# Where the product of px with the decays is made: one VectorE instruction, or four scaled copies on ScalarE

## The chip, the core and the metric

The kernel runs on one core of one Trainium2 chip, in one launch. The metric is the device time of that launch in microseconds (us), as a median over several runs. The core has five engines with queues of their own, each of which runs its instructions in the order of the program: TensorE (PE in the profile; its weight loads are PEld), VectorE (DVE), ScalarE (ACT), GpSimd (POOL) and SyncE (SP), which here only issues DMAs. They wait for one another through semaphores. Matmuls write to PSUM, of which a tile of 128 x 512 floats fills one bank; everything else that the engines share lies in SBUF.

## What is computed

The reference is one block of a network: layer norm, an attention layer, a residual sum, layer norm, a feed-forward layer with weights from a table of 16 values, a residual sum. The attention layer is a gated delta rule with 32 value heads of width 128 over 4 sequences of 1024 rows, in chunks of 64 rows. What matters here, cut from it (one head, one chunk; `Tm` is the inverse of a triangular matrix):

```python
u = Tm @ v_beta
kcd = Tm @ (k_beta * jnp.exp(gc)[..., None])
def step(St, inp):
    q_i, k_i, u_i, kcd_i, dec_i, g_i = inp
    attn = (q_i @ k_i.T) * dec_i
    v_new = u_i - kcd_i @ St
    inter = (q_i * jnp.exp(g_i)[..., None]) @ St
    out_i = inter + attn @ v_new
    g_last = g_i[..., -1]
    St_new = St * jnp.exp(g_last) + (k_i * jnp.exp(g_last - g_i)[..., None]).T @ v_new
    return St_new, out_i
```

So the new values of a chunk, `v_new`, are used twice: by the chunk's own output, and, scaled row by row with the decay from that row to the chunk's end, by the sum that updates the state `St`.

## The kernel before

**Tiling.** Heads are worked in 8 groups of 4. A *unit* is one chunk of two sequences for the 4 heads of a group: 2 x 64 rows fill the 128 partitions, and the 4 heads lie beside each other, 128 columns each, in one tile of 128 x 512 (`t4`, one PSUM bank). Eight units make a *super*; there are 4 supers in a group, 32 supers and 256 units in all. Units alternate between two pairs of sequences, so there are two running states, `S`.

**The order of the work** is written out by hand. `SLOTS` (lines 859 to 868) has one line for each unit of a super; each letter resumes one generator, and what it records goes at once to the end of the queues of the engines that it uses. In the order of a slot:

- `A` and `B`: `channel`, the projections of one tile of values (`A`) and of queries or keys (`B`) with a convolution: 8 matmuls `pp`, a scaled copy `cv` on ACT (line 437), three multiply-adds `cv` on DVE (line 440), a Silu on ACT (line 444).
- `N0`, `N1`, `N2`, `O3`, `J`, `O4`: the six parts of `step`, one unit. `N0` transposes the values (`pv`) and copies them, scaled, to `x0` on ACT (line 675). `N1` multiplies queries and keys with the state (`pkqs`), adds to `x0` on DVE (line 695) and makes `qs` on ACT (line 696: four copies, one for each head, scaled by a column). `N2` multiplies `x0` with the inverse: `px`, which is minus `v_new`, up to the scales; from it ACT makes `xs` (line 709), and line 712 makes `yg`, its product with the decays `ncd`; PE transposes the keys (`pk`), ACT copies them to `kt` (line 717), and POOL multiplies the state with its decay (line 721). The next unit's slot goes on: `O3` makes `po` from `xs` and `core` on DVE, `J` four sums of squares on ACT (`junk`), `O4` multiplies `kt` with `yg` (`pu`) and DVE adds that to the state (line 748).
- `T`, `Z`, `U`: `project_out`: gates (`pz`, a Silu `zs` on ACT, two products `zs` on POOL, lines 784 and 786), transposes (`pto`, `oT`), the output projection (`pout`, `ac`).
- `v1`: one step of `invert`, an inversion by substitution on DVE, two instructions with all operands in SBUF (`rank` and `v`, lines 580 and 581), 31 steps a super, spread over units 7 and 0 to 3 mostly.
- `n`, `s`, `b`, `r`, `q`: `norms`, `scores` (decays `dc` on POOL and ACT), `build`, `rms`, `roots`. In the slots with `r` and `q` ACT needs Sqrt and then Exp, and Silu again after that, and a table is loaded for each.

**Buffers.** Tiles from `bank` share four PSUM banks in turn: a matmul into the fifth tile waits until the readers of the first are done. In most slots the tiles come as px, pk, pout, po, pv, pto, pkqs, pkqs, pz (and kkq or others between), so `pz` takes the bank of `pv`, which is free when `x0` has been copied. Tiles `pp` and `pu` share two double banks. `px` is read twice, by `xs` and by `yg`, and its bank is free after both; the two readers run one after the other.

**What the change touches:** line 712 in `step`. `ncd` is a small tile made by `norms`, one column for each head of each unit; `bc` repeats a column along 128 elements. `last` is true in the last two units of a group, where there is no state to update; so line 712 runs in 240 of the 256 units.

Of the kernel before, what the change touches and what calls it, by code (L numbers as in the profile page):

```python
# [11 lines left out]
AF = mybir.ActivationFunctionType  # L12
ALU = mybir.AluOpType
# [10 lines left out]
HG = 4  # L24
# [35 lines left out]
def bc(ap, shape):  # L60
    return ap.to_broadcast(shape)
# [3 lines left out]
def delta_net_ffn_kernel(  # L65
# [18 lines left out]
    V, A, G_, T_ = nc.vector, nc.scalar, nc.gpsimd, nc.tensor  # L84
# [7 lines left out]
    def bank(name):  # L92
        return psum.tile([P, 512], F32, tag="ps", name=name)

    def two_banks(name):
        return psum2.tile([P, 2, 512], F32, tag="pp", name=name)
# [97 lines left out]
    with tc.tile_pool(name="pre", bufs=2) as pre, tc.tile_pool(name="gates", bufs=1) as gp:  # L194
# [38 lines left out]
        u = gp.tile(full, F32, name="u")  # L233
# [75 lines left out]
    with ExitStack() as main:  # L309
# [6 lines left out]
        def t4(name, bufs=1):  # L316
            return sc.tile([P, HG, P], F32, tag=name, name=name, bufs=bufs)

        h4 = [P, HG, P]

        def as4(ps):
            return ps.rearrange("p (h i) -> p h i", h=HG)
# [335 lines left out]
        def step(k, u):  # L658

            blk, un = divmod(u, 4)  # L660
            n, p = divmod(un, 2)
            ti = k.t0 + u
            ex, _, _, _, el = dks[k.g]
            first = k.first and u < 2
            last = k.last and u >= SB - 2
            S_ = states[p]
            qk, vt = k.qku.pop(u), k.vt[blk]

            pv = bank("pv")
            for h in range(HG):  # L670
                T_.transpose(as4(pv)[:, h, :], vt[h][:, un * P : (un + 1) * P], ident)
            x0 = t4("x0")
            for m in range(MG):
                two = slice(2 * m, 2 * m + 2)
                A.activation(x0[:, two, :], as4(pv)[:, two, :], AF.Copy, scale=k.nnk[:, u, m : m + 1])
            yield
            if not first:
                got = []
                for j in range(2):
                    ps = bank("pkqs")  # L680
                    for m in range(MG):
                        two = slice(2 * m, 2 * m + 2)
                        for ab in range(2):
                            T_.matmul(  # L684
                                as4(ps)[ab * C : (ab + 1) * C, two, :],
                                lhsT=qk[:, m, j, ab, :],
                                rhs=S_[:, ab, two, :],
                                start=True,
                                stop=True,
                            )  # L690
                    got.append(ps)
                qs = t4("qs")
                for h in range(HG):
                    e = ex[:, ti, h : h + 1]
                    V.scalar_tensor_tensor(x0[:, h, :], as4(got[0])[:, h, :], e, x0[:, h, :], ALU.mult, ALU.add)
                    A.activation(qs[:, h, :], as4(got[1])[:, h, :], AF.Copy, scale=e)
            yield

            ue, ae = k.exp.pop(u)

            def applied(w, src, name):
                ps = bank(name)
                for h in range(HG):
                    T_.matmul(as4(ps)[:, h, :], lhsT=w[:, h, :], rhs=src[:, h, :], start=True, stop=True)  # L704
                return ps

            px = applied(ue, x0, "px")
            xs = t4("xs")
            A.activation(xs, as4(px), AF.Copy, scale=-1.0)  # L709
            if not last:  # L710
                yg = t4("yg")
                V.tensor_tensor(yg, as4(px), bc(k.ncd[:, u, :].unsqueeze(2), h4), ALU.mult)
                pk = bank("pk")
                for m in range(MG):
                    T_.transpose(as4(pk)[:, m, :], qk[:, m, 0].rearrange("p a t -> p (a t)"), ident)
                kt = sc.tile([P, MG, P], F32, tag="kt", name="kt")
                A.copy(kt, as4(pk)[:, :MG, :])
                if not first:
                    flat = S_.rearrange("p a h d -> p (a h) d")
                    decay = el[:, ti].rearrange("p a h -> p (a h)").unsqueeze(2)  # L720
                    G_.tensor_tensor(flat, flat, bc(decay, [P, 2 * HG, P]), ALU.mult)  # L721
            yield
            po = applied(ae, xs, "po")
            core = t4("core", OUT_LAG)
            if first:
                V.tensor_copy(core, as4(po))
            else:
                V.tensor_tensor(core, as4(po), qs, ALU.add)  # L728
            k.cores[u] = core
            yield  # L730
            junk = sc.tile([P, P], F32, tag="junk", name="junk")
            for h in range(HG):
                A.activation(junk, core[:, h, :], AF.Square, accum_out=k.ms[:, u, h : h + 1])  # L733
            yield
            if not last:
                pu = two_banks("pu")
                for m in range(MG):
                    two = slice(2 * m, 2 * m + 2)
                    for ab in range(2):
                        half = slice(ab * C, (ab + 1) * C)  # L740
                        T_.matmul(  # L741
                            as4(pu[:, ab])[:, two, :], lhsT=kt[half, m, :], rhs=yg[half, two, :], start=True, stop=True
                        )
                state = S_.rearrange("p a h d -> p (a h d)")
                if first:
                    V.tensor_copy(state, pu.rearrange("p a n -> p (a n)"))
                else:
                    V.tensor_tensor(state, pu.rearrange("p a n -> p (a n)"), state, ALU.add)
# [274 lines left out]
        with tc.manual_schedule(engines=COMPUTE):  # L1023
            for s in range(-LQ, len(units)):
                n, i = divmod(s, SB)
                nq, iq = divmod(s + LQ, SB)
                nv, iv = divmod(s + LV, SB)
                gens = {}
                newer = step(*units[s]) if s >= 0 else None
                for c in "01234":  # L1030
                    gens["N" + c], gens["O" + c] = newer, older
# [127 lines left out]
```

## Time and profile before

| | us |
|---|---|
| median of 3 runs | 4344.73 |
| lowest and highest run | 4342.15 to 4349.24 |
| the profiled execution | 4347.06 |
| its span on the core | 4345.3 |
| chain that ended last: PE, DVE, ACT | 57%, 25%, 6% of the span |
| PE idle ahead of `px` (line 704) | 168.2 |
| DVE idle ahead of `cv` (line 440), until ACT's `cv` (line 437) | 322.7 |
| ACT idle ahead of `cv` (line 437), until PE's `pp` | 486.0 |

How to read it: the time of the runs holds a little more than the span, which goes from the first to the last instruction on the core. The chain is followed back from the last instruction, at each step to what released it or to its predecessor on its engine. Idle time of an engine that is not the bottleneck costs nothing. A row of a group reads: line, engine, operation, output<-inputs, shape, count | busy us, mean ns of one | idle us just before them, and what ended most of it. A row of the timeline reads: start us, length us, engine, line, operation, output<-inputs, shape, count, and in brackets the engine's idle time just before it with what ended that. A row of the windows reads: from:to, length, then for each engine its busy time and number of instructions, the granted clock of TensorE, the share of the DMA engines and GB/s.

### The profile page before, as it was taken

The numbers are of one execution on the slowest core, as the hardware profiler recorded it, in microseconds if no ns is written. First come the engines' busy times: TensorE is split into PE (matmuls) and PEld (weight loads), VectorE is DVE, ScalarE is ACT, GpSimd is POOL, SyncE is SP. The second block draws the span as 40 slices with busy tenths as digits, with TensorE's granted clock in tenths as the row PEclk, the third lists the DMA queues.
The fourth block names the chain that finished last, engine by engine and source line by source line (L and its number), as shares of the span: only waits on it lengthen the run. The fifth ranks groups of instructions, "written<-read, shape, count | busy, mean of one in ns | idle before, by whom it ended". The sixth has DMA issues, their size and how long they took to land.

```text
span 4345.3 us, 79442 instructions
## 1 busy us (share of the span) xinstructions
PE 3992.3 (92%) x26664; PEld 2858.5 (66%) x26664; DVE 3517.0 (81%) x6641; ACT 2646.9 (61%) x6573; POOL 2082.5 (48%) x1782
## 2 busy tenths in 40 slices
PE   3679999999999999999999999999999999999999
PEld 3456667677666666676766667676766776666454
DVE  4788888888888888888888988888888898886243
ACT  2456667666666666666666666666666666656211
POOL 2545564655555554655455554555554343434122
PEclk7899999999999999999999999999999999999999
DMA  3444444444444454444454444544445444443011
GB/s 88 124 107 113 111 112 124 121 130 119 126 130 118 107 133 125 134 117 119 125 135 128 109 114 128 133 118 114 132 128 128 115 120 121 130 108 96 26 39 29
DMA packets 1053124, 492.72 MB, mean 113 GB/s; under 512 B 730528, under 2 KB 951856, under 8 KB 1052720
## 3 DMA queue, kind: packets, MB, share of 16 engines
q1 hardware_dynamic: 1052720, 487.64, 42.5%
q8 instruction: 216, 3.54, 0.3%
q14 instruction: 188, 1.54, 0.1%
HBM read 267.66 MB, written 219.69 MB: 112 GB/s over the span
## 4 chain that ended last, share of the span: by engine, by line
PE 57%; DVE 25%; issue 7%; ACT 6%; POOL 3%; DMA 1%; SPq 1%; DVEq 0%; POOLq 0%; ACTq 0%
PE pp L423 13%; DVE cv L440 9%; PE pout L797 7%; PE pz L143 7%; PE pkqs L684 6%; DVE rank L580 4%; PE pgu L960 4%; PE px L704 4%; PE pu L741 3%; PE po L704 3%; DVE v L581 2%; PE kkq L546 2%; PE py L976 2%; DVE core L728 2%; PE pto L790 1%
## 5 line engine op out<-in xcount | busy, mean ns | idle before, releaser
L440 DVE SCALAR_TENSOR_TENSOR cv<-pp,cw,cv 128x512 f32<-128x512 f32 x1536 | 1148.9, 748 | 352.2 <-ACT cv L437 322.7
L784 POOL TENSOR_TENSOR zs<-zs,rr 128x512 f32<-128x512 f32 x256 | 267.0, 1043 | 1558.3 <-ACT zs L782 1549.3
L437 ACT ACTIVATE cv<-pp,cw 128x512 f32<-128x512 f32 x512 | 350.9, 685 | 486.0 <-PE pp L423 486.0
L581 DVE TENSOR_TENSOR v<-v,rank 128x31 f32<-128x31 f32 (+15 forms) x992 | 553.3, 558 | 34.1
L423 PE MATMUL pp<-xnT,wq 128*128 128x262 f32 x2048 | 531.0, 401 | 43.3 <-DVE cv L440 34.6
L423 PEld LDWEIGHTS pp<-xnT,wq 128*128 128x128 f32 x2048 | 371.7, 191 | 216.6 <-issue 58.7
L423 PE MATMUL pp<-xnT,wv 128*128 128x262 f32 x2048 | 503.0, 387 | 5.8 <-DVE cv L440 5.8
L797 PE MATMUL pout<-wo,oT 128*128 128x256 f32 x2048 | 504.9, 391 | 0.7 <-ACT oT L792 0.7
L143 PE MATMUL pz<-wzs,xnT 128*64 128x512 f32 x2048 | 487.1, 596 | 4.7 <-DVE ac L802 3.8
L580 DVE TENSOR_TENSOR rank<-v,lb 128x31 f32<-128x31 f32 (+15 forms) x992 | 467.2, 471 | 25.9 <-DMA lb<-ltd 20.1
L684 PE MATMUL pkqs<-S,qku 128*64 128x256 f32 x3840 | 478.1, 387 | 5.2 <-DVE core L728 3.5
L721 POOL TENSOR_TENSOR S<-S,dkm 128x1024 f32<-128x1024 f32 x224 | 436.7, 1949 | 26.5 <-PE pkqs L684 16.1
L704 PE MATMUL px<-x,ue 128*128 128x128 f32 x2048 | 292.9, 287 | 168.2 <-issue 108.1
L704 PEld LDWEIGHTS px<-x,ue 128*128 128x128 f32 x2048 | 264.1, 194 | 269.0 <-issue 151.1
L423 PEld LDWEIGHTS pp<-xnT,wv 128*128 128x128 f32 x2048 | 381.5, 190 | 73.8 <-issue 13.1
L797 PEld LDWEIGHTS pout<-wo,oT 128*128 128x128 f32 x2048 | 384.1, 198 | 49.4 <-issue 3.4
L684 PEld LDWEIGHTS pkqs<-S,qku 128*64 128x64 f32 x3840 | 248.7, 136 | 204.2 <-issue 49.2
L733 ACT ACTIVATE junk<-core 128x128 f32<-128x128 f32 x1024 | 318.5, 311 | 82.4 <-DVE core L728 53.9
L786 POOL TENSOR_TENSOR zs<-zs,core 128x512 f32<-128x512 f32 x256 | 328.6, 1284 | 20.0
L709 ACT ACTIVATE xs<-px 128x512 f32<-128x512 f32 x256 | 154.8, 605 | 236.2 <-PE px L704 236.2
L444 ACT ACTIVATE qk<-cv 128x512 f32<-128x512 f32 x256 | 161.2, 630 | 206.1 <-DVE cv L440 202.6
L741 PE MATMUL pu<-yg,kt 64*128 64x256 f32 x1920 | 272.2, 402 | 14.5 <-DVE cv L440 13.1
(187 smaller groups left out, 7198.4 us busy)
## 6 DMA issues: line engine op xcount, KB each, us to landing
qkd<-qk SPq DMA_DIRECT2D x256, 256.0 KB, 2.6
qku<-qkd SPq DMA_DIRECT2D x256, 256.0 KB, 2.9
dc<-rows_d SPq DMA_DIRECT2D x256, 128.0 KB, 3.4
ltd<-lT SPq DMA_DIRECT2D x128, 256.0 KB, 2.5
atd<-aT SPq DMA_DIRECT2D x128, 256.0 KB, 2.8
ae<-atd SPq DMA_DIRECT2D x512, 64.0 KB, 2.6
acc_d<-ac SPq DMA_DIRECT2D x256, 128.0 KB, 2.2
ac<-acc_d SPq DMA_DIRECT2D x224, 128.0 KB, 2.6
```

Of the source, the lines that this page charges most:

```text
L143: T_.matmul(ps[ab * C : (ab + 1) * C, :], lhsT=xnT[:, kc, 2 * p + ab, H + n * C : H + (n + 1) * C], rhs=rhs(kc), start=kc == 0, stop=kc == ...
L423: T_.matmul(ps[:, 2 * p : 2 * p + 2, : H + BT], lhsT=wt[:, kc, :], rhs=xnT[:, kc, 2 * p : 2 * p + 2, c0 : c0 + H + BT], start=kc == 0, sto ...
L437: A.activation(cv, ps[:, :, H : H + BT], AF.Copy, scale=cw[:, ch, H : H + 1])
L440: V.scalar_tensor_tensor(cv, ps[:, :, i : i + BT], cw[:, ch, i : i + 1], cv, ALU.mult, ALU.add)
L580: V.tensor_tensor(t, bc(v[:, 0 : j + 1, j : j + 1], sh), bc(lb[:, j : j + 1, j + 1 :], sh), ALU.mult)
L581: V.tensor_tensor(v[:, 0 : j + 1, j + 1 :], v[:, 0 : j + 1, j + 1 :], t, ALU.subtract)
L684: T_.matmul(as4(ps)[ab * C : (ab + 1) * C, two, :], lhsT=qk[:, m, j, ab, :], rhs=S_[:, ab, two, :], start=True, stop=True,)
L704: T_.matmul(as4(ps)[:, h, :], lhsT=w[:, h, :], rhs=src[:, h, :], start=True, stop=True)
L721: G_.tensor_tensor(flat, flat, bc(decay, [P, 2 * HG, P]), ALU.mult)
L741: T_.matmul(as4(pu[:, ab])[:, two, :], lhsT=kt[half, m, :], rhs=yg[half, two, :], start=True, stop=True)
L786: G_.tensor_tensor(zs, zs, k.cores.pop(u), ALU.mult)
L797: T_.matmul(pp[:, :HID], lhsT=oT[:, h, :], rhs=wo[:, h, :], start=h == 0, stop=h == HG - 1)
```

## The change

The one DVE instruction that multiplies all four heads of `px` with their decays becomes four ACT instructions, one for each head, in the same place of the program: each copies 128 x 128 elements of `px` with the head's column of `ncd` as scale. The values of `yg` stay the same.

```diff
             A.activation(xs, as4(px), AF.Copy, scale=-1.0)
             if not last:
                 yg = t4("yg")
-                V.tensor_tensor(yg, as4(px), bc(k.ncd[:, u, :].unsqueeze(2), h4), ALU.mult)
+                for h in range(HG):
+                    A.activation(yg[:, h, :], as4(px)[:, h, :], AF.Copy, scale=k.ncd[:, u, h : h + 1])
                 pk = bank("pk")
```

## The prediction, made before the changed kernel ran

> **What bounds the kernel now.** Names: a super is eight units (0 to 7) of one group of heads; "interval k" runs from the matmuls `px` of unit k to those of the next unit, so it holds N2 of unit k, then O3, J and O4 of k and N0 and N1 of k+1. First I read the busy times of the page:
>
> ```profile
> PE 3992.3 (92%) x26664; PEld 2858.5 (66%) x26664; DVE 3517.0 (81%) x6641; ACT 2646.9 (61%) x6573; POOL 2082.5 (48%) x1782
> ```
>
> PE is nearly full, so what counts is where PE stands still. The waits say that it does so mostly ahead of `px`: 168 us in all. The chain of waits gives PE 57% and DVE 25%. An average over units with different limits decides nothing, so I asked for the busy times of one super, one row for each interval: 5, 6, 7, 0, 1, 2, 3, 4 from top to bottom.
>
> ```profile
> core 0: us, PE busy (x) PEld busy (x) DVE busy (x) ACT busy (x) POOL busy (x), PEclk, DMA share, GB/s
> 2006.96:2020.83 13.87, 13.87 (x100) 10.70 (x99) 9.89 (x17) 10.50 (x25) 7.40 (x7) 1.00 0.68 190
> 2020.83:2037.32 16.49, 16.49 (x155) 11.19 (x153) 9.42 (x21) 10.64 (x27) 6.08 (x7) 1.00 0.63 156
> 2037.32:2053.72 16.40, 13.77 (x90) 10.01 (x87) 15.95 (x26) 8.53 (x23) 12.71 (x12) 1.00 0.36 89
> 2053.72:2070.73 17.01, 15.88 (x98) 11.88 (x99) 16.52 (x31) 12.83 (x28) 8.87 (x8) 0.90 0.28 68
> 2070.73:2086.20 15.47, 14.11 (x99) 10.62 (x99) 15.12 (x30) 8.77 (x24) 6.25 (x6) 1.00 0.43 127
> 2086.20:2100.36 14.16, 14.16 (x91) 9.81 (x91) 13.50 (x31) 7.64 (x23) 2.41 (x2) 1.00 0.57 174
> 2100.36:2113.89 13.53, 13.53 (x90) 10.26 (x87) 12.10 (x24) 8.76 (x24) 11.69 (x10) 1.00 0.29 77
> 2113.89:2128.58 14.69, 14.46 (x101) 10.68 (x100) 14.06 (x24) 13.04 (x30) 7.68 (x8) 1.00 0.40 107
> ```
>
> After the bounds stand the length, then PE's busy time. Five intervals are PE's own. In intervals 7, 0 and 1 (rows 3 to 5) DVE is full and PE stands still ahead of the next `px`: 2.6, 1.1 and 1.4 us here. Unit by unit the timeline repeats this in each group's second, third and fourth super (22 of them outside the kernel's end): 2.6, then 1.1 to 2.1, then 1.4 us; a group's first super has only the last, 2.5 us. ACT is loaded in intervals 0 and 4 alone (12.83 of 17.01 and 13.04 of 14.69), where three table loads of 1.28 us stand on it.
>
> **The change part by part.** The program's order shows one move: 240 `yg` leave DVE, and 960 copies stand on ACT between `xs` and `kt`; every other instruction keeps its place, on SP and POOL too, and no DMA is moved. The prices:
>
> ```profile
> L696 ACT ACTIVATE qs<-pkqs,dkm 128x128 f32<-128x128 f32 x960 | 269.9, 361 | 0.5 <-PE pkqs L684 0.5
> L712 DVE TENSOR_TENSOR yg<-px,ncd 128x512 f32<-128x512 f32 x240 | 164.0, 683 | 25.6 <-ACT xs L709 23.1
> ```
>
> L696 is the same operation in the same shape: PSUM in, SBUF out, scale from a column, four in a row. Four take 1.12 us in the timeline, and the next instruction starts 1.00 us after the first of them. So ACT's queue moves by 1.00 us in each unit (upper bound 4 x 361 ns = 1.44, if nothing overlapped; nothing on ACT is removed, so there is no gain there to bound). DVE's queue gets 0.60 us, the step from `yg` to its successor. Where is either on the path?
>
> *Interval 4, ACT.* The two `x0` copies (L675) free the bank that `pz` writes:
>
> ```profile
> 2117.47 0.21 ACT L765 ACTIVATE rr<-rr 128x16 f32<-128x16 f32 x1 [0.33 <-DVE rr L763]
> 2122.92 0.83 ACT L675 ACTIVATE x<-pv,nnk 128x256 f32<-128x256 f32 x2
> 2123.80 0.20 PEld L143 LDWEIGHTS pz<-wzs,xnT 128*64 128x64 f32 x4 [0.37 <-ACT x L675]
> ```
>
> From `xs` to `x0` ACT has no idle time but the 0.33 us before `rr`. `pz` starts 0.05 us after `x0` ends in 28 supers; behind it on PE are `kkq`, `pp` and `px` of unit 5. In 15 of them the 0.33 us are missing and the delay is 1.00, in 13 it is 0.68: 15 x 1.00 + 13 x 0.68 = 24 us lost. In the other intervals `pz` has 0.5 to 2.3 us of room.
>
> *Interval 0, ACT.* Here ACT is full too. DVE's first `cv` step of the next value channel starts 0.27 us after ACT made that `cv`:
>
> ```profile
> 2061.67 0.67 ACT L437 ACTIVATE cv<-pp,cw 128x512 f32<-128x512 f32 x1
> 2062.61 2.31 DVE L440 SCALAR_TENSOR_TENSOR cv<-pp,cw,cv 128x512 f32<-128x512 f32 x3
> ```
>
> One microsecond later on ACT makes DVE stand 0.76 us longer than now, though its queue is 0.60 us shorter (`core` ends early and waits). From there DVE runs without a break to `x0` (L695), which `px` of unit 1 waits for. ACT's own tail (`junk`, `vt`, `qs`, `zs`, no idle time) brings POOL's `zs` products 0.83 to 1.00 late, and they hold DVE (next paragraph). I take 0.95 x 22 supers = 21 us lost; bounds 0.76 x 22 = 17 and 1.44 x 22 = 32.
>
> *Interval 7, DVE.* One would count 0.60 us won ahead of `px` of unit 0. But DVE is behind POOL there:
>
> ```profile
> 2038.86 1.90 POOL L721 TENSOR_TENSOR S<-S,dkm 128x1024 f32<-128x1024 f32 x1
> 2039.39 0.68 DVE L712 TENSOR_TENSOR yg<-px,ncd 128x512 f32<-128x512 f32 x1
> 2039.99 0.90 DVE L580 TENSOR_TENSOR rank<-v,lb 128x112 f32<-128x112 f32 x1
> ...
> 1807.68 1.04 POOL L784 TENSOR_TENSOR zs<-zs,rr 128x512 f32<-128x512 f32 x1 [2.71 <-ACT zs L782]
> 1807.81 1.13 DVE L580 TENSOR_TENSOR rank<-v,lb 128x192 f32<-128x192 f32 x1
> 1808.80 1.26 POOL L786 TENSOR_TENSOR zs<-zs,core 128x512 f32<-128x512 f32 x1
> 1808.97 1.31 DVE L581 TENSOR_TENSOR v<-v,rank 128x192 f32<-128x192 f32 x1
> ```
>
> `yg` reads PSUM and runs at its usual 0.68 beside POOL's product. `rank` has both inputs in SBUF; it takes 0.90 instead of the 0.27 of the same shape at 2110.42, and ends 0.13 us after POOL does, and the next three of its kind do likewise. So without `yg` `rank` starts at 2039.39 and still ends at 2040.89: won 0 (bounds 0 and 0.60 x 22 = 13 us).
>
> *Interval 1, DVE.* `yg` sits between `cv` steps here, with no POOL product near; ACT has 2.25 us of idle time, which hides the copies. `core` and `vt` come 0.60 and 0.47 earlier; ACT's `zs` must then wait for `pz` (ends at 2082.00, `zs` starts at 2082.35 now): 0.35. POOL's `zs` products hold `rank` and `v` as above, so `px` of unit 2 comes 0.32 earlier: 22 x 0.32 = 7 us won (bounds 0 and 13).
>
> *Intervals 2, 3, 5, 6.* PE is the bound; ACT idles 2.85, 1.31, 0.90 and 2.13 us behind the copies, which covers 1.00 (without that cover it would be as in interval 4). *First super of each group:* `pto` and `pu` wait there for `yg` and for the `cv` behind it (1.2 us a group to be won), but POOL's `dc` products come 0.27 later and hold DVE: 0 (bounds 10 us won, 3 lost).
>
> **The sum.** +24 + 21 - 7 + 0 = +38 us on the profiled execution's 4347.06 us, so 4385. The three runs have a median of 4344.73, 2.3 lower: **4383 us**, +0.9%. Bounds of this case: all low ends, 24 + 17 - 13 - 13 - 10 = +5 (4350); copies at 1.44, 28 x 0.44 + 22 x 0.49 = +23 on top (4406).
>
> [...]
>
> **The rivals.**
> A, faster: DVE slips ahead of POOL. In interval 7 `rank` starts only 0.13 us after POOL's `zs` product; 0.60 us less on DVE could let `rank` and `v` run first, at 0.36 each instead of 1.13 and 1.31: 1.72 us; the same pair in interval 1 0.83 + 1.35 - 0.77 = 1.41. It decides from 45 us / 22 = 2.0 us a super on; in full it gives 24 + 21 - 22 x 3.13 = -24: 4321. Against it: POOL's `zs` follows ACT's `vt`, which waits for the same DVE steps and moves by 0.47 itself, so DVE gains only 0.13, and interval 7 is pinned before that.
> B, no change: no hold by POOL counts, DVE's 0.60 arrives whole in intervals 7 and 1 and in the groups: +5 to +9 us, 4351. For it: DVE is the engine in the chain there.
> C, slower still: the copies don't overlap, 1.44 us a unit: 4406. Against it: all 240 foursomes of L696 do.
> That the change isn't carried out is excluded by the program's order.
>
> **How the numbers follow.** Forecast 0.62, C 0.14, B 0.12, A 0.12. Less than 0.2% (9 us) can't be told from no change. Faster 0.12 (A), same 0.12 (B), slower 0.76. The range 4342 to 4406 holds the forecast with its bounds, B and C's edge.
>
> **What would show it.** In the profile after: `pz` about 0.9 us later after `px` in interval 4, still released by ACT `x0`; the stall ahead of `px` of unit 1 near 3.1 and 2.1, of unit 0 still 2.6, of unit 2 about 1.1; four copies in 1.12 us; ACT near 2917 us busy, DVE near 3353 less what POOL's holds change. Wrong if the stall of unit 0 shrinks by over 0.5 us, or if `pz` isn't later.

## The result, and the profile after

| | before | after |
|---|---|---|
| median, us (4 runs each) | 4344.59 | 4387.59 |
| lowest and highest run | 4342.15 to 4349.24 | 4384.32 to 4393.37 |
| span of the profiled execution | 4345.3 | 4386.4 |
| ratio of the times, 95% interval | | 1.0099 [1.0082, 1.0117] |

The changed kernel is 43.0 us slower by the medians and 41.1 by the spans. (Behind line 712 its line numbers are one higher.) First the page of the changed kernel: the busy times, the chain by engines, and two groups of instructions (busy us, mean ns of one, idle us before them and what ended it).

```profile
PE 4022.2 (92%) x26664; PEld 2892.3 (66%) x26664; DVE 3375.4 (77%) x6401; ACT 2891.2 (66%) x7533; POOL 2077.2 (47%) x1782
...
PE 73%; ACT 11%; DVE 9%; issue 4%; DMA 1%; POOL 1%; SPq 0%; ACTq 0%; DVEq 0%; POOLq 0%
...
L440 DVE SCALAR_TENSOR_TENSOR cv<-pp,cw,cv 128x512 f32<-128x512 f32 x1536 | 1150.0, 749 | 482.1 <-ACT cv L437 446.7
L143 PE MATMUL pz<-wzs,xnT 128*64 128x512 f32 x2048 | 490.9, 600 | 47.4 <-ACT x L675 38.1
```

DVE has 142 us less to do, ACT 244 more. DVE's gain went into waiting: ahead of `cv` it now stands 446.7 us until ACT's `cv` comes, against 322.7 before. PE, which waited 4.7 us in all ahead of `pz` by the page of before, now waits 47.4, of which 38.1 end with ACT's `x0`. In the chain DVE fell from 25% to 9% and ACT rose from 6% to 11%. The row of `pz` in the page of before:

```profile
L143 PE MATMUL pz<-wzs,xnT 128*64 128x512 f32 x2048 | 487.1, 596 | 4.7 <-DVE ac L802 3.8
```

The windows of the changed kernel, for the same super as in the prediction, again one row for each interval 5, 6, 7, 0, 1, 2, 3, 4:

```profile
2030.78:2044.65 13.87, 13.87 (x100) 10.69 (x98) 9.29 (x16) 11.40 (x29) 7.40 (x7) 1.00 0.67 185
2044.65:2061.14 16.49, 16.49 (x155) 11.19 (x153) 8.82 (x20) 11.67 (x31) 6.09 (x7) 1.00 0.64 157
2061.14:2077.54 16.40, 13.78 (x90) 10.01 (x87) 15.95 (x25) 9.46 (x27) 12.71 (x12) 1.00 0.35 88
2077.54:2095.31 17.77, 15.88 (x99) 11.89 (x99) 14.89 (x30) 13.76 (x32) 8.43 (x8) 0.90 0.28 66
2095.31:2110.93 15.62, 15.62 (x98) 12.14 (x99) 14.55 (x32) 9.29 (x27) 4.97 (x5) 0.89 0.46 134
2110.93:2125.01 14.08, 14.08 (x91) 9.73 (x89) 13.43 (x27) 9.31 (x28) 3.95 (x3) 1.00 0.57 166
2125.01:2138.55 13.54, 13.54 (x90) 10.26 (x87) 12.06 (x23) 9.80 (x28) 11.68 (x10) 1.00 0.30 76
2138.55:2153.80 15.25, 14.09 (x99) 10.60 (x98) 12.40 (x24) 14.08 (x34) 7.52 (x8) 1.00 0.42 109
```

Set these lengths beside those of before. Intervals 5, 6, 7, 2 and 3 are as they were to within 0.08 us. Interval 0 (row 4) went from 17.01 to 17.77, with DVE less busy (16.52 to 14.89) and ACT fuller. Interval 4 (row 8) is 15.25 against 14.53 from `px` to `px` (the row shown of before ran 0.16 us past that `px`; the row without them is below). Interval 1 (row 5) went from 15.47 to 15.62; there PE is now busy all the time, at a granted clock of 0.89 instead of 1.00, to which the last section returns.

```profile
2113.89:2128.42 14.53, 14.30 (x99) 10.52 (x98) 13.90 (x24) 13.04 (x30) 7.52 (x8) 1.00 0.40 107
```

The timeline of the changed kernel (start us, length us, then the idle time in brackets) at the three places of the prediction, interval 7, 0 and 4:

```profile
2062.69 1.90 POOL L722 TENSOR_TENSOR S<-S,dkm 128x1024 f32<-128x1024 f32 x1
2062.83 1.14 ACT L713 ACTIVATE yg<-px,ncd 128x128 f32<-128x128 f32 x4
2063.22 1.50 DVE L580 TENSOR_TENSOR rank<-v,lb 128x112 f32<-128x112 f32 x1
2063.83 0.40 ACT L718 COPY kt<-pk 128x256 f32<-128x256 f32 x1
...
2086.53 0.67 ACT L437 ACTIVATE cv<-pp,cw 128x512 f32<-128x512 f32 x1
2087.23 2.32 DVE L440 SCALAR_TENSOR_TENSOR cv<-pp,cw,cv 128x512 f32<-128x512 f32 x3 [1.38 <-ACT cv L437]
...
2142.85 0.22 ACT L766 ACTIVATE rr<-rr 128x16 f32<-128x16 f32 x1
2148.30 0.83 ACT L675 ACTIVATE x<-pv,nnk 128x256 f32<-128x256 f32 x2
2149.18 1.94 PE L143 MATMUL pz<-wzs,xnT 128*64 128x512 f32 x8 [1.16 <-ACT x L675]
```

Lines 1 to 4: without `yg`, `rank` begins earlier and takes 1.50 us instead of 0.90; it ends at 2064.72, 0.13 us after POOL's product, just as before, and 3.58 us after `px` where it was 3.57. Its relief is gone at once. The four copies take 1.14 us, and `kt` starts 1.00 after the first of them. Lines 5 and 6: ACT's `cv` starts 8.99 us after `px` of unit 0 (before: 7.95), and DVE stands 1.38 us for it. Lines 7 to 9: `rr` no longer waits, `x0` ends at 2149.13, and `pz` starts 0.05 us later.

### The profile page after: what moved, and what is told of

It is laid out like the page before. It is cut to its first block, busy times and chain, and to the rows that moved or that the text cites. A ratio compares the mean times of both kernels' runs of the same rounds, so it can differ in the third digit from the quotient of the medians.

```text
span 4386.4 us, 80207 instructions
## 1 busy us (share of the span) xinstructions
PE 4022.2 (92%) x26664; PEld 2892.3 (66%) x26664; DVE 3375.4 (77%) x6401; ACT 2891.2 (66%) x7533; POOL 2077.2 (47%) x1782
## 4 chain that ended last, share of the span: by engine, by line
PE 73%; ACT 11%; DVE 9%; issue 4%; DMA 1%; POOL 1%; SPq 0%; ACTq 0%; DVEq 0%; POOLq 0%
PE pp L423 17%; PE pz L143 9%; PE pout L798 9%; PE pkqs L684 8%; PE px L704 6%; PE pu L742 4%; PE po L704 4%; PE pgu L961 4%; DVE cv L440 3%; PE kkq L546 2%; PE pto L791 2%; PE py L977 2%; PE pv L671 2%; DVE rank L580 2%; ACT cv L437 2%
## 5 line engine op out<-in xcount | busy, mean ns | idle before, releaser
L440 DVE SCALAR_TENSOR_TENSOR cv<-pp,cw,cv 128x512 f32<-128x512 f32 x1536 | 1150.0, 749 | 482.1 <-ACT cv L437 446.7
L423 PE MATMUL pp<-xnT,wq 128*128 128x262 f32 x2048 | 531.9, 402 | 44.1 <-DVE cv L440 34.9
L581 DVE TENSOR_TENSOR v<-v,rank 128x31 f32<-128x31 f32 (+15 forms) x992 | 526.0, 530 | 34.1
L143 PE MATMUL pz<-wzs,xnT 128*64 128x512 f32 x2048 | 490.9, 600 | 47.4 <-ACT x L675 38.1
L798 PE MATMUL pout<-wo,oT 128*128 128x256 f32 x2048 | 531.6, 407 | 0.8 <-ACT oT L793 0.7
L423 PE MATMUL pp<-xnT,wv 128*128 128x262 f32 x2048 | 504.9, 388 | 5.3 <-DVE cv L440 5.3
L684 PE MATMUL pkqs<-S,qku 128*64 128x256 f32 x3840 | 469.3, 386 | 0.0
L722 POOL TENSOR_TENSOR S<-S,dkm 128x1024 f32<-128x1024 f32 x224 | 437.2, 1952 | 25.6 <-PE pkqs L684 21.0
L798 PEld LDWEIGHTS pout<-wo,oT 128*128 128x128 f32 x2048 | 403.1, 207 | 56.5 <-issue 3.4
L143 PEld LDWEIGHTS pz<-wzs,xnT 128*64 128x64 f32 x2048 | 143.2, 138 | 245.8 <-issue 149.9
```

Source lines behind the costliest of these rows:

```text
L143: T_.matmul(ps[ab * C : (ab + 1) * C, :], lhsT=xnT[:, kc, 2 * p + ab, H + n * C : H + (n + 1) * C], rhs=rhs(kc), start=kc == 0, stop=kc == ...
L423: T_.matmul(ps[:, 2 * p : 2 * p + 2, : H + BT], lhsT=wt[:, kc, :], rhs=xnT[:, kc, 2 * p : 2 * p + 2, c0 : c0 + H + BT], start=kc == 0, sto ...
L440: V.scalar_tensor_tensor(cv, ps[:, :, i : i + BT], cw[:, ch, i : i + 1], cv, ALU.mult, ALU.add)
L581: V.tensor_tensor(v[:, 0 : j + 1, j + 1 :], v[:, 0 : j + 1, j + 1 :], t, ALU.subtract)
L684: T_.matmul(as4(ps)[ab * C : (ab + 1) * C, two, :], lhsT=qk[:, m, j, ab, :], rhs=S_[:, ab, two, :], start=True, stop=True,)
L798: T_.matmul(pp[:, :HID], lhsT=oT[:, h, :], rhs=wo[:, h, :], start=h == 0, stop=h == HG - 1)
```

## The experiments

Ten kernels ran, in three groups, each beside the kernel before, which took 4345.41 us (with e1 to e4), 4345.23 us (e5, e6, e8) and 4345.30 us (e9 to e11). e4 leaves the product `yg` out and e6 one product of the state with its decay; these two serve to measure time alone. The table has their medians, ratios and, from the profiled executions, the sum over all supers of each interval's change of length against before (from `px` to `px`, read from the timeline; intervals 3, 5 and 6 change by under 3 us everywhere). Interval 2's changes are mostly whole stretches of half clock of PE (3.41 us at a granted clock of 0.5, so 1.7 us lost in each) that the groups' first supers get or don't; the last section returns to them.

| kernel | us | ratio, 95% interval | int. 0 | 1 | 2 | 4 | 7 |
|---|---|---|---|---|---|---|---|
| the changed kernel | 4387.59 | 1.0099 [1.0082, 1.0117] | +24.6 | -5.0 | -2.6 | +25.9 | -0.8 |
| e1: DVE in units 0 and 4 | 4334.53 | 0.9972 [0.9962, 0.9982] | +3.7 | -11.0 | -0.6 | -2.8 | -1.1 |
| e2: ACT in unit 4 only | 4375.62 | 1.0071 [1.0058, 1.0084] | +0.5 | +0.5 | -1.2 | +25.6 | -0.4 |
| e3: ACT in unit 0 only | 4380.60 | 1.0080 [1.0067, 1.0094] | +34.9 | -4.9 | -1.9 | +2.6 | -0.7 |
| e4: no product | 4329.60 | 0.9961 [0.9949, 0.9974] | -4.8 | -9.3 | +1.8 | -2.5 | -1.1 |
| e5: copies of `px` beside the product | 4414.40 | 1.0160 [1.0146, 1.0174] | +27.2 | +2.1 | -5.0 | +27.0 | +11.8 |
| e10: copies of `xs` beside the product | 4415.58 | 1.0165 [1.0151, 1.0179] | +39.2 | -1.6 | -5.8 | +36.5 | 0.0 |
| e6: no decay in unit 7 | 4308.17 | 0.9912 [0.9899, 0.9926] | +11.2 | +1.4 | -6.7 | +3.2 | -48.3 |
| e8: ACT in unit 1 only | 4334.49 | 0.9974 [0.9964, 0.9984] | +0.7 | -10.1 | -5.0 | 0.0 | -0.5 |
| e9: unit 7's decay on ACT | 4310.90 | 0.9923 [0.9910, 0.9935] | +11.8 | +0.2 | -6.3 | +2.1 | -48.0 |
| e11: e8 and e9 together | 4306.75 | 0.9913 [0.9898, 0.9928] | +11.9 | -4.5 | -0.5 | +2.0 | -48.3 |

### Where is the loss? The change in some units alone

e1 keeps the copies in all units but the two in which the prediction found a loss.

```diff
-                for h in range(HG):
-                    A.activation(yg[:, h, :], as4(px)[:, h, :], AF.Copy, scale=k.ncd[:, u, h : h + 1])
+                if u not in (0, 4):
+                    for h in range(HG):
+                        A.activation(yg[:, h, :], as4(px)[:, h, :], AF.Copy, scale=k.ncd[:, u, h : h + 1])
+                else:
+                    V.tensor_tensor(yg, as4(px), bc(k.ncd[:, u, :].unsqueeze(2), h4), ALU.mult)
```

> The product is made by four copies on ACT in units 1, 2, 3, 5, 6 and 7 of each super (176 times), and by the one DVE instruction, as before, in units 0 and 4 (64 times). Theory (ACT's queue is on the path only in intervals 0 and 4, where it is full): both losses go, intervals 0 and 4 have the lengths of before, interval 1 stays 0.3 us shorter: 4332 to 4342 us, ratio 0.997 to 0.9995. Rival 'every copy costs': the loss of 43 us is spread over the 240 units and 176/240 of it stay, 4376 us, ratio 1.007. Rival 'clock' (the loss comes from the half-clock records that the profile shows more of): no gain beyond what fewer such records give; their number, 37 long pout after the change against 15, must then fall together with the time.

The loss is gone and a small gain stays: 176 of the 240 foursomes (the four copies of one unit) cost nothing. e2 and e3 do the reverse, with `if u == 4` and `if u == 0` in the place of `if u not in (0, 4)`.

> Four copies on ACT in unit 4 alone (32 of 240), the rest as before. Theory: interval 4 is 0.72 or 1.03 us longer in 28 supers as it is after the whole change, since pz waits for x0 behind the copies: +25 us, 4370, ratio 1.0058. Rival 'every copy costs': 32/240 of 43 us, +6, 4350, ratio 1.0013. Rival 'clock': the number of long pout stays near 15, so no change, ratio 1.000.

> Four copies on ACT in unit 0 alone (32 of 240), the rest as before. Theory: interval 0 is about 1.0 us longer in the 22 supers in which px of unit 1 waits, +21 to +25 us, 4368, ratio 1.0055. Rival 'every copy costs': +6, 4350, ratio 1.0013. Rival 'DVE is the bound there' (DVE's 0.6 us free in interval 0 is worth what it was meant to be): -0.6 x 22 = -13, 4331, ratio 0.997.

Each of the two has its loss in its own interval and changes no other by 5 us or more. e2 gives 25.6 us in interval 4, the changed kernel 25.9. (e2's medians differ by more, 30.2 us; its profiled execution, 4372.42 us, is the fastest of its five.) e3 lost more than expected. The windows of e3's interval 0 in supers 14 and 15, counted from 0 (length, then PE, PEld, DVE, ACT, POOL, the granted clock, the DMA share, GB/s), and then the timeline at the beginning of the second:

```profile
1949.54:1967.29 17.75, 14.41 (x99) 10.62 (x99) 14.79 (x30) 13.74 (x32) 8.41 (x8) 1.00 0.28 66
2071.74:2090.35 18.61, 15.74 (x98) 11.89 (x99) 14.91 (x30) 13.74 (x32) 8.44 (x8) 0.92 0.27 63
```

```profile
2071.74 2.05 PE L704 MATMUL px<-x,ue 128*128 128x128 f32 x8 [2.62 <-issue]
2073.82 0.60 ACT L709 ACTIVATE xs<-px 128x512 f32<-128x512 f32 x1 [3.98 <-PE px L704]
```

Thirteen of the 22 ordinary supers (not the first of a group) look like the second row: the eight matmuls of `px` take 1.70 to 2.05 us instead of 1.22, at half clock, and with ACT full behind them the whole interval is later by up to 0.86. The other nine have 17.75, near the prediction's +0.95 a super. In the changed kernel the half clock mostly fell on `pout` instead (531.6 us busy, 504.9 before), where PE had idle time that took most of it up. So the parts don't add up: e1, e2 and e3 against 4345.41 are -10.9, +30.2 and +35.2, 54.5 together, and the whole change costs 43.0.

The rival 'clock' falls with e1 and e2. Between 300 and 4000 us the profile shows 15 stretches of half clock before and 38 in the changed kernel; e2 has 18 and loses 25.6 us in interval 4 all the same, and e1 has 23, more than before, and is faster than before. In e3 the clock does add to the loss, as just shown.

### What is DVE's relief worth by itself?

e4 takes `yg` from DVE without giving it to ACT.

```diff
+        zero = w1.tile(h4, F32, tag="yg0", name="yg0")
+        G_.memset(zero, 0.0)
...
-                yg = t4("yg")
-                V.tensor_tensor(yg, as4(px), bc(k.ncd[:, u, :].unsqueeze(2), h4), ALU.mult)
+                yg = zero
```

> Nobody makes the product: the update of the state multiplies the keys with a tile of zeros, and DVE's instruction is left out without anything put on ACT. What is left is DVE's relief alone, 0.6 us in each of 240 units. Theory: ahead of px of unit 0 nothing is won, since POOL's products hold DVE (the stall stays 2.6 us); interval 1 wins 0.3 to 0.5 us, interval 0 between 0 and 0.6 us, the groups' first supers up to 1.2 us each: 4318 to 4338, ratio 0.994 to 0.9985, and the stall of unit 0 unchanged. Rival 'DVE is the bound in intervals 7, 0 and 1': 0.6 x 66 = -40 and the groups -10: 4295, ratio 0.9885, and the stall of unit 0 falls to 2.0 us.

240 instructions of 683 ns less on DVE, 164 us, bring 15.8 us. The stall ahead of `px` of unit 0 is 59.0 us over all supers, against 59.6: interval 7 isn't shortened by DVE's relief. That was rival A's point of decision, and 0.60 us a super doesn't reach it.

### Where is that gain won?

```diff
+                if u == 1:
+                    for h in range(HG):
+                        A.activation(yg[:, h, :], as4(px)[:, h, :], AF.Copy, scale=k.ncd[:, u, h : h + 1])
+                else:
+                    V.tensor_tensor(yg, as4(px), bc(k.ncd[:, u, :].unsqueeze(2), h4), ALU.mult)
```

> Four copies on ACT in unit 1 alone, the product on DVE in all others. Theory (what the kernel with copies in six units won is won in interval 1 alone): -0.3 us in each of 22 ordinary supers and -0.5 us in each group's first super, 8 to 11 us less, about 4335 us, ratio near 0.9977. Rival (that gain is spread over its six units): -2 us, ratio 0.9996. Second rival (every four copies cost time): ratio 1.0013.

e8 with 32 foursomes reaches e1's time with 176: the gain is interval 1's, -0.29 us in each ordinary super (predicted: -0.32) and -3.2 us in the groups' first supers.

### ACT's load without DVE's relief

e5 makes the copies as well as the product, into a tile that nothing reads. e10 is the same with `xs` in the place of `as4(px)`, and with the product recorded ahead of the copies.

```diff
                 yg = t4("yg")
+                yo = t4("yo")
+                for h in range(HG):
+                    A.activation(yo[:, h, :], as4(px)[:, h, :], AF.Copy, scale=k.ncd[:, u, h : h + 1])
                 V.tensor_tensor(yg, as4(px), bc(k.ncd[:, u, :].unsqueeze(2), h4), ALU.mult)
```

> DVE keeps the product yg as before, and ACT makes the same four scaled copies in the same place as in the changed kernel, into a tile that nothing reads: ACT's load alone, without DVE's relief. Theory (the loss is ACT's queue in intervals 4 and 0, the relief of DVE is worth about 16 us elsewhere, as the kernel without any product showed): interval 4 +25 us, interval 0 +24 to +35, nothing won in interval 1 and in the groups' first supers, so +50 to +57 us, about 4398 us, ratio near 1.0125. Rival (DVE's relief is worth nothing while ACT is so loaded): the time of the changed kernel, ratio 1.0099. Second rival (the loss comes from yg coming later to PE, not from ACT's queue): ratio 1.000, since yg is made by DVE as before.

> As the kernel with the copies beside the product, but the four copies that nothing reads take xs instead of px, so that DVE's yg no longer waits for them (with copies of px, yg began up to 1.03 us later than before after xs). Theory (the extra loss of that kernel was this lateness of yg; ACT's load alone costs interval 4 +25 and interval 0 +24 to +35 us): interval 7 as before, +50 to +58 us in all, about 4399 us, ratio near 1.0125. Rival (ACT's load costs that much by itself as long as DVE isn't relieved): 4414 us, ratio 1.016, interval 7 +12 us. Second rival (DVE's relief is worth nothing beside a loaded ACT): ratio 1.0099.

Both missed the theory's number, each for a cost that its edit brought with it. In the groups of instructions of e5 (first) and e10:

```profile
L714 ACT ACTIVATE yo<-px,ncd 128x128 f32<-128x128 f32 x960 | 275.0, 382 | 0.0
L715 DVE TENSOR_TENSOR yg<-px,ncd 128x512 f32<-128x512 f32 x240 | 164.3, 685 | 112.7 <-ACT yo L714 112.5
```

```profile
L715 ACT ACTIVATE yo<-xs,ncd 128x128 f32<-128x128 f32 x960 | 308.3, 393 | 7.8
L712 DVE TENSOR_TENSOR yg<-px,ncd 128x512 f32<-128x512 f32 x240 | 164.0, 683 | 25.9 <-ACT xs L709 23.4
```

In e5 the readers of `px` run one after the other, so DVE's `yg` waits 112.5 us for the copies, where it waited 23.1 for `xs`; that is the +11.8 in interval 7, which e10 doesn't have. By the spans e5 is 66.5 us above before; without the 11.8 it is 55, which the theory had, and 14 more than the 41.1 of the changed kernel. That is near what e4 won (17.5 by its span).

In e10 the copies read SBUF. The first of them starts 0.63 us after `xs` starts, against 0.49 in the changed kernel, and the step of four is 1.19 us against 1.00, so `kt` comes 0.33 us later in each unit. In the 28 supers of interval 4 and the 22 of interval 0 that is, as an estimate, 16 us of the 72.4 by which e10's span is above before's; the 56 that are left are 15 more than the changed kernel's 41.1. e10's time, 4415.58 us, is near the 4414 of its rival, but the rival's +12 in interval 7 is absent. That is a rough account, from two kernels that each changed more than one thing; but that the loss comes from ACT's queue, not from a late `yg`, e10 shows, since there `yg` is made by DVE and waits 23.4 us for `xs`, where it waited 23.1 before.

### What holds interval 7?

Two edits of the kernel before at line 721, e6 and e9; e11 is e9 with e8's edit.

```diff
-                if not first:
+                if not first and u != 7:
```

```diff
                     decay = el[:, ti].rearrange("p a h -> p (a h)").unsqueeze(2)
-                    G_.tensor_tensor(flat, flat, bc(decay, [P, 2 * HG, P]), ALU.mult)
+                    if u == 7:
+                        for j in range(2 * HG):
+                            A.activation(flat[:, j, :], flat[:, j, :], AF.Copy, scale=decay[:, j])
+                    else:
+                        G_.tensor_tensor(flat, flat, bc(decay, [P, 2 * HG, P]), ALU.mult)
```

> The kernel before, with the product of the state and its decay (POOL, line 721) left out in unit 7 of each super; everything else as before. Theory (POOL's products hold DVE's rank and v in interval 7, so DVE's own queue isn't the only bound there): rank beside the left-out product takes 0.3 us instead of 0.9, POOL's later products come earlier, and the stall ahead of px of unit 0 falls from 2.6 us to 0.5 to 1.5; 24 to 45 us less, 4300 to 4320 us, ratio 0.990 to 0.9945. Rival (POOL holds nothing, DVE's queue alone sets interval 7): stall 2.6 us as before, ratio 1.000. Between them (the hold by line 721 is made up for by the later products of POOL): stall 2.0 to 2.6 us, ratio 0.9965 to 1.000.

> The kernel before, with the product of the state and its decay of unit 7 made by ACT (eight copies of 128x128, scaled by a column) instead of by POOL. Theory (the product on POOL holds DVE; ACT idles 2.53 us behind kt and qk in interval 7, which covers eight copies at a step of 0.25 us = 2.0 us): as without that product, stall ahead of px of unit 0 near 0.6 us, 4308 to 4318 us, ratio 0.991 to 0.994. Rival (what ACT makes next is late by 2.0 us instead, and the stall stays): stall 2.0 us or more, ratio 0.998 to 1.006.

> Both of the gains: unit 7's decay on ACT, and the four copies on ACT in unit 1 alone. Theory (they are in different intervals, 7 and 1, and add): the kernel with the decay on ACT less about 10 us, ratio 0.988 to 0.9915. Rival (the second gain isn't there once px of unit 0 comes earlier, because POOL and ACT then set interval 1): no lower than the kernel with the decay on ACT alone.

e6 takes nothing from DVE's queue and makes interval 7 2.1 to 2.2 us shorter ahead of nearly every ordinary super, over three times the 0.60 us of `yg`, of which nothing came through. Two places of e9's timeline show how, the first behind `px` of unit 7, the second ahead of `px` of unit 0:

```profile
2026.71 0.37 ACT L717 COPY kt<-pk 128x256 f32<-128x256 f32 x1
2026.96 2.46 ACT L723 ACTIVATE S<-S,dkm 128x128 f32<-128x128 f32 x8
2027.69 1.40 POOL L531 TENSOR_TENSOR dc<-dc,above 128x512 f32<-128x512 f32 x1
2027.70 0.27 DVE L580 TENSOR_TENSOR rank<-v,lb 128x112 f32<-128x112 f32 x1
2028.00 1.23 DVE L581 TENSOR_TENSOR v<-v,rank 128x112 f32<-128x112 f32 x1
...
2037.44 0.35 DVE L580 TENSOR_TENSOR rank<-v,lb 128x192 f32<-128x192 f32 x1
2037.54 1.15 POOL L788 TENSOR_TENSOR zs<-zs,rr 128x512 f32<-128x512 f32 x1 [3.98 <-ACT zs L786]
2037.83 1.08 DVE L581 TENSOR_TENSOR v<-v,rank 128x192 f32<-128x192 f32 x1
...
2039.27 0.96 PE L704 MATMUL px<-x,ue 128*128 128x128 f32 x6 [0.54 <-issue]
```

`rank` of 112 elements takes 0.27 us instead of 0.90, and much later `rank` of 192 elements starts 0.10 us ahead of POOL's `zs` product, takes 0.35 instead of 1.13, and POOL's product is the longer one, 1.15 instead of 1.04. DVE has slipped ahead of POOL, as rival A said it might if it were far enough forward. The stall ahead of `px` falls from 2.63 to some 0.6. e9's eight copies stand on ACT for 2.46 us in time that it had to spare. e9 beats the kernel before by 34.4 us and the changed one by 77. e11 is the fastest of all, 38.6 us below the kernel before, but the ratios' intervals of e9 and e11 overlap and its gain in interval 1 is only 4.5 us instead of 10.1: the two gains don't add up. Interval 0 became 11 to 12 us longer in all three. What bounds it then wasn't tried.

## Why the prediction was right, point by point

*Interval 4: +24, measured +25.9.* `pz` starts 0.05 us after `x0` ends, before and after. It came 9.60 us after `px` in 15 supers and 9.91 in 13; now it is 10.63 in all 28. That is 1.03 and 0.72 where 1.00 and 0.68 were put, and 25 us in all. e2 shows it alone.

*Interval 0: +21, measured +24.6*, of which the 22 ordinary supers give 0.93 each (put: 0.95) and the groups' first supers 4.3, where nothing was put. The place is as predicted: DVE waits for ACT's `cv`, and its own `cv` starts 9.69 us after `px` of unit 0 in the super shown instead of 8.89, 0.80 later where 0.76 was put. One expected sign failed here: the stall ahead of `px` of unit 1 was to be near 3.1 and 2.1 us, and is 1.9 to 2.6. In the eight ordinary supers whose `pout` behind `px` of unit 0 took 1.89 us before and is drawn out to 2.65 to 3.50 now, that stall changed by -0.2 to +0.5 us, while the interval grew by 1.0 to 1.7. So the mean of 0.93 is also no cleaner than that: where no stretch of half clock lies in the interval before or after (supers 13, 17 and 19) it is +1.02 to +1.07. The interval's length is the measure, not that one stall.

*Interval 7: 0, measured -0.8.* In the super shown `rank` ends 0.13 us after the product on POOL, before and after; the stall of unit 0 is still 2.6 us. e4 and e9 show it from both sides: DVE's relief does nothing there, POOL's does 2.1 us a super.

*Interval 1: -7, measured -5.0, but not where it was put.* In six ordinary supers the interval went from 15.46 to 15.55 us down to 15.21, as predicted; in the other 16 it is 0.04 to 0.20 longer, and the stall ahead of `px` of unit 2, put at 1.1 us, is 0. In those, `pout` runs at half clock for most of its length (2.45 to 3.58 us instead of 1.89), PE becomes the bound, and the 0.3 us are gone. The -5.0 come from the groups' first supers (-5.3), for which 0 was put together with their other intervals; those lose 4.3 in interval 0, so that the 0 holds only as a sum. The term was right in sum by luck, by two errors that cancel. e8, where interval 0 isn't touched, has the -0.29 a super.

*The price of the copies.* The step of 1.00 us for four was right. Rival C (1.44) falls with it. The step is 1.00 in this trace, where the copies read PSUM, and 1.19 in e10, where they read SBUF. The move from VectorE cost time in units 0 and 4 (e3 35.2 us, e2 30.2), but in unit 1 e8 is 10.7 us faster with the copies on ScalarE.

*The busy times.* ACT was put near 2917 us and DVE near 3353; they are 2891.2 and 3375.4. The prediction had added and taken off whole busy times of groups, but neighbours on an engine overlap: four copies of 380 ns on average, 1.52 us in all, stand on ACT for 1.14. The changes, 244 and 142 us, are near 240 times the steps of 1.00 and 0.60 us.

*The rivals.* A's mechanism exists, as e9 shows, but 0.60 us doesn't reach its point of decision. B let DVE's relief arrive whole: 13 us in interval 7, 13 in interval 1 and 10 in the groups' first supers, 36 in all. In e4 the whole relief is worth 15.8, and none of it arrives in interval 7.

The sum was 4383 us, the time is 4387.59: 38 predicted, 43.0 found. By the table interval 0 lost 3.6 us more than was put, interval 4 1.9 more, interval 1 won 2.0 less, and interval 2, put at nothing, won 2.6.

## What to carry to other kernels

Ask for each unit of a loop which engine is late there, and price a move stage by stage: the same four copies cost 0.7 to 1 us in units 0 and 4, nothing in 2, 3, 5, 6 and 7, and gain 0.3 us in unit 1. Relief of a busy engine was worth nothing where its next instruction was held by another engine (in interval 7, a stall of 59.0 us in e4 against 59.6); move the work that holds it instead, here one POOL product to ACT, which had 2.5 us to spare, for 34 us. And a queue without idle time between two releases (ACT from `xs` to `x0` in 15 supers of interval 4) handed on everything that was put into it, 1.03 us for a step of 1.00.

## What the hardware showed unexpectedly

**After 46 of 100 TensorE stalls of over 1.85 us its granted clock fell to 0.5.** The timeline of the changed kernel at the beginning of interval 1 of the super shown above:

```profile
2095.31 1.44 PE L704 MATMUL px<-x,ue 128*128 128x128 f32 x8 [1.89 <-issue]
...
2096.97 3.10 PE L798 MATMUL pout<-wo,oT 128*128 128x256 f32 x8
```

After 1.89 us of idle time `pout` takes 3.10 us instead of 1.89, and the window's clock is 0.89. Between 300 and 4000 us the clock's records in the two traces show 15 stretches of half clock before (27 us of clock lost) and 38 after (65 us). Their starts lie on one grid of 3.413 us, to 1% of a step, in both executions, and all but one last one step. After 130 PE stalls of 0.7 to 1.85 us, before and after together, one such stretch began within 1.6 us; after 100 stalls of over 1.85 us, 46. Which of the long stalls is followed by one depends on where they lie on the grid: of the 48 that ended at most 1.6 us ahead of a grid point 46 were followed at that point, of the other 52 none, and of 78 short ones that ended as close to one, 1. So neighbouring supers get it in the same place and a kernel some microseconds longer gets it elsewhere: in e3 it sat on `px`, for 0.8 us a super, in the changed kernel on `pout`. That accounts for most of the 10 us that e3 loses in interval 0 beyond the changed kernel, and so for why the parts don't add up. The long stalls that were followed by a stretch lasted 1.88 to 2.63 us. Why the clock falls there, no run shows.

**`rank` and `v`, which have two operands in SBUF, took longer beside POOL's instructions.** Of 1984 `rank` and `v` before, the 760 that overlap with a POOL instruction take 795 ns on average, the 1224 others 340 (331 for the same mix of shapes). `yg`, which reads PSUM, takes 0.68 us beside POOL (148 of them, 685 ns on average) and without (92, 681 ns). Which of the two starts first mostly decides which is drawn out: the 51 that start ahead of a POOL product take at most 4% more than without one, and of the 525 that start behind one 86% take over 20% more. In e9 0.10 us of start decides between 0.35 and 1.13 us for `rank`.
